# A gated MLP that takes its image by pairs of chunks, in one core of a four-layer network

## The chip, the core and the metric

The kernel runs on one core of one Trainium2 chip. The core has five engines that each take their own list of instructions in the order in which it is written: TensorE (PE; matmuls, with PEld for its weight loads), VectorE (DVE), ScalarE (ACT), GpSimd (POOL), and SyncE (SP), which here only issues DMAs. They wait for each other through semaphores. Data lies in SBUF, 128 partitions wide; matmuls write to PSUM[...].

The metric is the time of one execution on the device in microseconds (us), and its median over runs. All data is float32.

## The reference

Four images of 192 channels and 64 x 64 pixels pass through four layers: L0, an attention over channels with a deformable convolution, and an MLP; L1, an attention over all pixels; L2, an attention in overlapping windows, then a gate and a gated MLP; L3, a convolution with weights made from the image's mean. The change lies in the second half of L2 and touches L3:

```python
out = _hft(_conv1x1(out, proj_w, proj_b), hft_w, hft_b)   # sigmoid(dwconv3(3x - three poolings of x)) * x
x1 = x + out
z = jax.nn.gelu(_conv1x1(_ln_c(x1, n2g, n2b), fc1_w, fc1_b), approximate=False)
z1, z2 = jnp.split(z, 2, axis=1)
z = z1 * _dwconv3(_ln_c(z2, sgn_g, sgn_b), sg_w, sg_b)
return x1 + _conv1x1(z, fc2_w, fc2_b)
```

`_ln_c` is a layer norm over the channels of each pixel, `fc1` goes from 192 to 768 channels, `z1` and `z2` have 384, `_dwconv3` is a 3 x 3 convolution of each channel by itself (nine taps), and `fc2` goes back to 192. L3 then gives each channel four taps of its own image: left, and three of the row above.

## The kernel before, in words

**Order of the whole.** For each image b: `layer1`, with the gathers of image b+1 woven in; `windows` (L2's attention); then `rest(b)`, which runs `project` (the gate `_hft`), `mlp` (the gated MLP) and `layer3`. For images 0 to 2, `rest` also carries `mlp0(b+1)`, L0's MLP of the next image. After `rest`, `keys` and, for some images, `offsets` prepare the next `layer1`.

**How `mlp0` is woven in.** `mlp0` is a generator. It has 33 parts: one to begin, then four for each of 8 chunks. I call them A (`attend` of the next chunk and `widen` of groups 0, 1), B (mean and square of the next chunk's norm, `widen` 2, 3), C (`widen` 4, 5, the norm's variance and reciprocal, `narrow(1)`) and D (the norm's product, `narrow(0)`, the store). `project`, `mlp` and `layer3` yield numbers; each full 1.0 of their sum lets `mlp0` issue its next part there. What is left is issued after `layer3`. Image 3 has nothing beside it (`alone`).

**What sets the order.** Inside `with tc.manual_schedule()`, which encloses the rounds of `mlp`, every engine has the instructions in the order of the program, the parts of `mlp0` that are issued there included. Elsewhere a planner orders them by readiness; it may also put later work, such as `keys`, between the instructions of `mlp`.

**Layout of the image.** `x` holds channels 0 to 127 on the 128 partitions, 4096 pixels long, and channels 128 to 191 on 64 partitions: the upper half of the image (chunks 0 to 3) on partitions 0 to 63, the lower half (4 to 7) on 64 to 127 (`upper_of`). A chunk is 8 rows, 512 pixels, one PSUM bank.

**`project`** works on six units of 1024 elements: units 0 to 3 are channels 0 to 127 of 16 rows each, 4 and 5 the channels above of two halves. `first(u)` projects and pools, `second(u)` does the nine taps, the sigmoid and two products. The halo rows of a unit are copied by POOL, or by two DMAs where they change partitions (`share`).

**`mlp`** goes by chunks, in ten rounds i: chunk i is widened and gated, chunk i+1 is normed, and the taps and the second matmul of chunk i-2 are done. In the order of the code: `taps_of(last, 0)`; `end()` (adds the second matmul of the round before to `x`, with sums for L3); `widen(i, (3, 4, 5))`, which makes `z2` and needs `hns[i]`, the normed chunk; the norm's mean; the gate's mean; the norm's difference and square; the gate's difference and square; `widen(i, (0, 1, 2))` for `z1`; `taps_of(last, 1)`; both variances and reciprocals; `taps_of(last, 2)`; a part of `mlp0`; the norm's product; `gate_scale`, after which ACT writes the gated rows to a strip and POOL copies halo rows (`share`); `narrow(last)`.

`widen` runs, for each of the groups m of 128 output channels, a matmul over 128 rows and one over 64 rows, those of the chunk's half; a matmul of float32 shows in the trace as two records. `narrow` runs three matmuls to 128 and three to 64 output channels. `taps_of` works on 512 columns of DVE: one multiplication and eight multiply-adds, then `z1 = (acc + b) * z1`. In image 3, two of the taps (`GATE_PE`) and five of the gate's in `project` (`HFT_PE`) are matmuls with diagonal matrices.

**PSUM in `rest`.** Tags: `n` (means, broadcasts), 2 banks; `v`, 1; `h` (widening, narrowing, and `mlp0`'s), 5, or in image 3 three, with two for `t` (taps on PE).

Of the kernel before, what the change touches and what calls it, by code (L numbers as in the profile page):

```python
# [79 lines left out]
def conv_seq_kernel(ctx: ExitStack, tc: tile.TileContext, a, out: bass.AP):  # L80
# [1197 lines left out]
    def strips(held):  # L1278


        tiles = {}

        def get(i):
            if i not in tiles:
                t = tiles[i] = held[:, i % held.shape[1]]
                nc.gpsimd.memset(t[:, :, :, 0:1], 0.0)
                nc.gpsimd.memset(t[:, :, :, W + 1 : W + 2], 0.0)
                if i == 0:
                    nc.gpsimd.memset(t[:, :, 0, 1 : W + 1], 0.0)
                if i == NCH - 1:  # L1290
                    nc.gpsimd.memset(t[:, :, 9, 1 : W + 1], 0.0)
            return tiles[i]

        def share(i):

            if i > 0:
                nc.gpsimd.tensor_copy(get(i - 1)[:, :, 9, 1 : W + 1], get(i)[:, :, 1, 1 : W + 1])  # L1297
                nc.gpsimd.tensor_copy(get(i)[:, :, 0, 1 : W + 1], get(i - 1)[:, :, 8, 1 : W + 1])

        return get, share  # L1300

    def depthwise_steps(strip, w, diag, taps, acc, ps, name):


        parts, rows = strip.shape[0], strip.shape[1] - 2
        acc = acc.rearrange("p (r c) -> p r c", c=W)

        def src(tap, r=0, n=rows):
            return strip[:, tap // 3 + r : tap // 3 + r + n, tap % 3 : tap % 3 + W]

        others = [tap for tap in range(9) if tap not in taps]
        first = others.pop(0)
        if taps:
            n = CN // W
            for r in range(0, rows, n):
                p = ps.tile([128, CN], F32, tag="t", name=f"{name}_{r}")[:parts]
                for j, tap in enumerate(taps):
                    nc.tensor.matmul(p, lhsT=diag[:, j, :], rhs=src(tap, r, n), start=j == 0, stop=j == len(taps) - 1)
                to, p = acc[:, r : r + n], p.rearrange("p (r c) -> p r c", c=W)
                nc.vector.scalar_tensor_tensor(to, src(first, r, n), w[:, first : first + 1], p, ALU.mult, ALU.add)  # L1320
        else:
            nc.vector.tensor_scalar_mul(acc, src(first), w[:, first : first + 1])
        for j, tap in enumerate(others):
            nc.vector.scalar_tensor_tensor(acc, src(tap), w[:, tap : tap + 1], acc, ALU.mult, ALU.add)  # L1324
            if j % 3 == 1:
                yield

    def depthwise(*args):
        links(depthwise_steps(*args))


    def upper_of(x, i):

        q, at = i // 4, 4 * UN + CN * (i % 4)
        rows = slice(Q * q, Q * q + Q)
        return x[:, bass.ts(i, CN)], x[rows, at : at + CN], rows

    def chunk_norm_steps(x, i, sb, ps, name):

        lo, hi, rows = upper_of(x, i)  # L1340
        pm = ps.tile([128, CN], F32, tag="n", name=f"pm_{name}")
        nc.tensor.matmul(pm, lhsT=mean_all[:, 0, :], rhs=lo, start=True, stop=False)
        nc.tensor.matmul(pm, lhsT=mean_all[rows, 0, :], rhs=hi, start=False, stop=True)
        yield MEAN
        d = sb.tile([M, 2, CN], F32, tag="ln_d", name=f"d_{name}", bufs=2)
        nc.vector.tensor_tensor(d[:, 0], lo, pm, ALU.subtract)
        nc.vector.tensor_tensor(d[rows, 1], hi, pm[rows], ALU.subtract)
# [405 lines left out]
    class Psums:  # L1753


        def __init__(self, pools):
            self.pools = pools
# [144 lines left out]
```

## Time and profile before

| | us |
|---|---|
| median of 3 runs (lowest, highest) | 7158.63 (7141.57, 7182.09) |
| the profiled execution, its own time | 7071.53 |
| its span, first to last instruction | 7069.4 |
| busy over the span: PE, DVE, ACT, POOL | 6342.5, 4928.1, 3763.7, 2122.6 |
| image 0: `project`, `mlp` | 1858.5 to 2025, 2025 to 2358 |
| image 1: `project`, `mlp`, `layer3` | 3513.7 to 3680, to 4010, to 4041 |
| image 2: `project`, `mlp` | 5170 to 5337, 5337 to 5665 |
| image 3: `project`, `mlp`, `layer3` | 6548 to 6641, to 7035, to 7069.4 |

The stage limits are read from the first and last instructions of the lines that belong to a stage. A stage's row gives, for each engine, its busy time and its number of instructions, then the share of the TensorE clock that was granted (PEclk), the mean share of the DMA engines, and the rate. Matmul records overlap a little, so a busy PE is not a PE at its peak. A row of a group gives line, engine, operation, output and inputs with their shapes, the count; then busy time and mean ns of one; then the idle time just before, and what ended it. A row of the chain gives start, duration, and the work.

### The profile page before, as it was taken

What the parts mean: (1) busy time and instruction counts of PE and PEld (TensorE: products, weight loads), DVE (VectorE), ACT (ScalarE), POOL (GpSimd) and SP (SyncE); (2) the same over time, 40 slices, a digit from 0 to 9 for tenths busy, and PEclk for the clock granted to TensorE, in tenths of its full rate; (3) what the DMA queues carried; (4) which work ended last, traced back from release to release, by engine and by line L of the source; (5) the groups of instructions that cost most, each with busy time, mean ns of one, the idle gap of its engine ahead of it and who ended that gap; (6) DMA issues with size and microseconds to landing.
All of it is one profiled execution on the core that took longest, in us unless ns stands there. A gap on an engine that the chain in (4) does not pass through costs nothing.

```text
span 7069.4 us, 116083 instructions
## 1 busy us (share of the span) xinstructions
PE 6342.5 (90%) x45368; PEld 4236.5 (60%) x45368; DVE 4928.1 (70%) x7476; ACT 3763.7 (53%) x6276; POOL 2122.6 (30%) x2352
## 2 busy tenths in 40 slices
PE   7878999999998799998999699998999889989876
PEld 4545688866553378885654358886654467756332
DVE  3763399955668579984678759994586967746555
ACT  3763388845453268874454258883544345535321
POOL 2761177732100067752200037771200000022100
PEclk8989999989999899998999899998999989989977
DMA  7993367630110377751010167762010010010000
GB/s 239 301 345 102 96 208 228 214 110 12 29 38 3 117 229 218 216 176 36 23 43 7 50 218 227 217 214 60 11 41 25 18 33 12 13 36 7 8 0 19
DMA packets 356994, 742.32 MB, mean 105 GB/s; under 512 B 47463, under 2 KB 241687, under 8 KB 355678
## 3 DMA queue, kind: packets, MB, share of 16 engines
q0 software_dynamic: 95040, 467.22, 20.7%
q1 hardware_dynamic: 261406, 267.69, 12.7%
q8 instruction: 357, 5.85, 0.3%
q14 instruction: 191, 1.56, 0.1%
HBM read 628.06 MB, written 106.21 MB: 104 GB/s over the span
## 4 chain that ended last, share of the span: by engine, by line
PE 45%; DVE 13%; ACT 3%; issue 2%; DMA 1%; POOL 1%; SPq 0%; DVEq 0%; ACTq 0%; POOLq 0%
PE s L910 8%; PE y L976 7%; DVE ga L1324 4%; PE h L590 3%; PE h L1494 3%; PE v L1136 2%; PE qk L1061 2%; PE qk L1062 1%; PE f L1547 1%; PE t L1144 1%; PE po L482 1%; PE zm L1506 1%; PE rb L1210 1%; PE o L818 1%; DVE top L917 1%
## 5 line engine op out<-in xcount | busy, mean ns | idle before, releaser
L572 POOL DMA_INDIRECT ring<-table,idx x1188 | 1696.2, 1428 | 1037.8 <-DMA wkT<-in_wkT_dram 234.6
L910 PE MATMUL s<-ths,ph 96*128 96x256 f32 x4096 | 977.0, 385 | 5.0 <-ACT ths L904 4.0
L910 PEld LDWEIGHTS s<-ths,ph 96*128 96x128 f32 x4096 | 781.8, 192 | 142.4 <-ACT ths L904 16.7
L578 ACT ACTIVATE row<-ring,pos 128x384 f32<-128x384 f32 x1188 | 699.6, 610 | 275.4 <-DVE xo L583 182.7
L579 DVE SCALAR_TENSOR_TENSOR row<-ring,fr,row 128x384 f32<-128x384 f32 x1188 | 700.8, 613 | 126.5 <-ACT row L578 119.8
L976 PE MATMUL y<-sc,gx 128*97 128x256 f32 x3008 | 723.3, 379 | 0.0
L976 PEld LDWEIGHTS y<-sc,gx 128*97 128x97 f32 x3008 | 489.5, 164 | 123.2 <-issue 1.1
L1324 DVE SCALAR_TENSOR_TENSOR ga<-gate,v,ga 128x512 f32<-128x512 f32 x720 | 541.4, 752 | 27.0
L582 ACT ACTIVATE xo<-row,pos 128x192 f32<-128x192 f32 x1188 | 505.3, 448 | 65.4 <-DVE row L579 33.6
L583 DVE SCALAR_TENSOR_TENSOR xo<-row,fr,xo 128x192 f32<-128x192 f32 x1188 | 465.5, 412 | 40.6 <-ACT xo L582 38.1
L590 PE MATMUL h<-ti,xo 128*128 128x192 f32 x2376 | 464.2, 329 | 6.3 <-DVE xo L583 6.3
L912 ACT COPY sc<-s 128x1024 f32<-128x1024 f32 x376 | 377.2, 1003 | 155.7 <-PE s L910 154.6
L973 DVE TENSOR_TENSOR sc<-sc,mbs 128x1024 f32<-128x1024 f32 x376 | 449.1, 1219 | 11.7 <-ACT mbs L936 11.3
L917 DVE TENSOR_TENSOR top<-top,sc 128x1024 f32<-128x1024 f32 x282 | 344.6, 1222 | 127.7 <-ACT sc L912 127.5
L590 PEld LDWEIGHTS h<-ti,xo 128*128 128x128 f32 x2376 | 405.4, 191 | 43.0 <-DVE xo L583 11.2
L974 ACT ACTIVATE sc<-sc 128x1024 f32<-128x1024 f32 x376 | 393.2, 1054 | 29.9 <-DVE sc L973 27.4
L1494 PE MATMUL h<-d_l2n,fc1T 128*128 128x512 f32 (+1 forms) x768 | 375.5, 630 | 34.0 <-DVE x L1555 31.5
L1120 DVE TENSOR_REDUCE es<-ex 128x6 f32<-128x384 f32 x264 | 133.3, 546 | 388.1 <-ACT ex L1116 388.1
L1297 POOL COPY gate<-gate 128x192 f32<-128x192 f32 x28 | 13.9, 497 | 1286.0 <-ACT gate L1528 1286.0
L590 PE MATMUL h<-kept,xo 128*128 128x192 f32 x990 | 253.5, 388 | 80.8 <-DVE xo L583 73.1
L1494 PEld LDWEIGHTS h<-d_l2n,fc1T 128*128 128x128 f32 (+1 forms) x768 | 143.6, 197 | 252.8 <-issue 189.2
L1547 PE MATMUL f<-z,fc2T 128*64 128x512 f32 (+1 forms) x384 | 222.6, 714 | 74.1 <-DVE z L1539 74.1
(376 smaller groups left out, 11409.9 us busy)
## 6 DMA issues: line engine op xcount, KB each, us to landing
ti<-table SPq DMA_DIRECT2D x396, 96.0 KB
table<-tt SPq DMA_DIRECT2D x24, 1056.0 KB
ring<-table,idx POOLq DMA_INDIRECT x1188
xnd<-xn SPq DMA_DIRECT2D x4, 3270.0 KB
table<-kept SPq DMA_DIRECT2D x12, 1056.0 KB
table<-tt SPq DMA_DIRECT2D x44, 288.0 KB
xi<-in_x_dram SPq DMA_DIRECT2D x32, 384.0 KB
xk<-xd SPq DMA_DIRECT2D x32, 384.0 KB
```

Source lines behind the costliest of these rows:

```text
L572: nc.gpsimd.indirect_dma_start(out=gt.rearrange("p r q c -> p (r q c)"), out_offset=None, in_=table[:, :], in_offset=bass.IndirectOffsetOn ...
L578: nc.scalar.activation(row, gt[:, :, 0, :], AF.Copy, scale=pos[:, t, 9 + tap : 10 + tap])
L579: nc.vector.scalar_tensor_tensor(row, gt[:, :, 1, :], fr[:, t, 9 + tap : 10 + tap], row, ALU.mult, ALU.add)
L582: nc.scalar.activation(xo[:, j, :], row[:, 0, :], AF.Copy, scale=pos[:, t, tap : tap + 1])
L583: nc.vector.scalar_tensor_tensor(xo[:, j, :], row[:, 1, :], fr[:, t, tap : tap + 1], xo[:, j, :], ALU.mult, ALU.add)
L590: nc.tensor.matmul(acc[m // 2][:, bass.ts(m % 2, C)], lhsT=xo.rearrange("p j c -> p (j c)")[:, bass.ts(m, 128)], rhs=tt, start=t == 0 and ...
L910: nc.tensor.matmul(p[:, t, :], lhsT=ph[:, bass.ts(G * g + t, 128)], rhs=ths[i], start=True, stop=True)
L917: nc.vector.tensor_tensor(tops[i], tops[i], to, ALU.max)
L973: nc.vector.tensor_tensor(ex, ex, mbs[i].unsqueeze(1).to_broadcast([128, G, QN]), ALU.add)
L976: nc.tensor.matmul(py, lhsT=gx[:, G * g + t, :], rhs=ex[:, t, :], start=g == 0 and t == 0, stop=g == NG - 1 and t == G - 1,)
L1324: nc.vector.scalar_tensor_tensor(acc, src(tap), w[:, tap : tap + 1], acc, ALU.mult, ALU.add)
L1494: nc.tensor.matmul(banks[m], lhsT=fc1b[of, k, bass.ts(m, 128)], rhs=hns[i][of, k, :], start=k == 0, stop=k == 1)
```

## The change

**Pairs.** `of_pair` takes two neighbouring chunks: channels 0 to 127 are 1024 elements of the 128 partitions; channels 128 to 191 of the first chunk lie on partitions 0 to 63 and those of the second on 64 to 127, in the same 512 columns. So `x`, `project`'s units 4 and 5 and the loads of the image are laid out anew. Units 4 and 5 become two blocks of 8 rows each, with halos across the halves of the partitions: 10 DMAs (before: 2 DMAs and two copies by POOL).

**The norm** is done for a pair at once (`pair_norm_steps`): one square, one variance, one root and one reciprocal of twice the size; subtractions and products stay four.

**The taps** run over 16 rows, 1024 columns. `depthwise_steps` is a generator that yields each tap, so that a group's taps are split: `upper_taps` does taps 0 to 5, which don't need the row below, `lower_taps` the last three and the product with `z1`.

**The round.** Five rounds instead of ten; the taps are one pair behind, `narrow` two pairs. The yields are placed anew, in `project` too (three of 0.5 for each `second`, where there were four of 0.83).

**PSUM.** Tag `t` is now `h`: five banks for both, in image 3 too.

```diff
+        yield first
+        for tap in others:
+            for b in range(blocks):
+                nc.vector.scalar_tensor_tensor(acc[:, b], src(tap, b), w[:, tap : tap + 1], acc[:, b], ALU.mult, ALU.add)
+            yield tap
...
+        lo, hi = of_pair(x, j)
+        pms = [ps.tile([128, CN], F32, tag="n", name=f"pm_{name}_{h}") for h in range(2)]
+        for h in range(2):
+            nc.tensor.matmul(pms[h], lhsT=mean_all[:, 0, :], rhs=lo[:, h], start=True, stop=False)
+        for h in range(2):
+            nc.tensor.matmul(pms[h], lhsT=mean_all[half(h), 0, :], rhs=hi[half(h)], start=False, stop=True)
...
+        sq = sb.tile([M, 3, CN], F32, tag="ln_sq", name=f"sq_{name}")
+        nc.scalar.activation(sq, d, AF.Square)
...
+                    moves = [
+                        (lo[:, :, 9, row], hi[:, :, 1, row]), (hi[:, :, 0, row], lo[:, :, 8, row]),
+                        (hi[:, 0, 9, row], lo[:, 1, 1, row]), (lo[:, 1, 0, row], hi[:, 0, 8, row]),
+                    ]
+                    if u == 5:
+                        over = get(4)[half(1), 1]
+                        moves += [(over[:, 9, row], lo[:, 0, 1, row]), (lo[:, 0, 0, row], over[:, 8, row])]
+                    for to, of in moves:
+                        nc.sync.dma_start(out=to, in_=of)
...
                     for _ in second(u):
-                        yield 0.83
+                        yield 0.5
...
+                banks = {(m, h): ps.tile([128, CN], F32, tag="h", name=f"h2_{b}_{j}_{m}_{h}") for m in ms for h in range(2)}
+                for (m, h), p in banks.items():
+                    nc.tensor.matmul(p, lhsT=fc1b[:, 0, bass.ts(m, 128)], rhs=hn[:, h], start=True, stop=False)
+                for (m, h), p in banks.items():
+                    nc.tensor.matmul(p, lhsT=fc1b[half(h), 1, bass.ts(m, 128)], rhs=hn[half(h), 2], start=False, stop=True)
...
+                p = ps.tile([128, CN], F32, tag="h", name=f"f2_{b}_{j}_2")
+                for m in range(3):
+                    for h in range(2):
+                        nc.tensor.matmul(
+                            p[half(h)], lhsT=fc2b[:, m, M:C], rhs=z1[:, m, bass.ts(h, CN)], start=m == 0, stop=m == 2
+                        )
...
+                for j in range(NCH // 2 + 1):
+                    gating, norming, last = j < NCH // 2, j + 1 < NCH // 2, j - 1
+                    lo, hi = 2 * j, 2 * j + 1
+                    if gating:
+                        widen(j, (3, 4))
+                    if last > 0:
+                        narrow(last - 1)
                     if last >= 0:
+                        upper_taps(last, 0)
                     end()
+                    if last >= 0:
+                        yield 1.0
+                    if not gating:
+                        lower_taps(last, 0)
+                        yield 1.0
+                    if gating:
+                        widen(j, (5, 0))
+                    if last >= 0:
+                        upper_taps(last, 1)
+                    if not gating:
+                        lower_taps(last, 1)
+                        yield 1.0
+                    yield 1.0
+                    if gating:
+                        gate_mean(lo)
+                        gate_mean(hi)
+                        gate_difference(lo)
+                        gate_square(lo)
+                        gate_difference(hi)
+                        widen(j, (1, 2))
+                        gate_variance(lo)
+                        gate_square(hi)
+                    if last >= 0:
+                        upper_taps(last, 2)
                     if not gating:
                         yield 1.0
+                        lower_taps(last, 2)
+                        yield 2.0
                     if gating:
+                        nc.vector.reciprocal(r[lo], r[lo])
+                        if last >= 0:
+                            yield 1.0
+                        gate_variance(hi)
+                        gate_scale(lo)
+                        nc.vector.reciprocal(r[hi], r[hi])
+                    if gating:
+                        if last >= 0:
+                            lower_taps(last, 0)
+                        gate_scale(hi)
                     if norming:
+                        norm = pair_norm_steps(x, j + 1, sb, ps, f"l2n2_{b}_{j + 1}")
+                        links(norm, SQUARE)
                     if gating:
+                        if last >= 0:
+                            lower_taps(last, 1)
                         yield 1.0
                     if norming:
+                        links(norm, INVERSE)
                     if gating:
+                        if last >= 0:
+                            lower_taps(last, 2)
                     if norming:
+                        hns[j + 1] = links(norm)
+                    hns.pop(j, None)
+                narrow(NCH // 2 - 1)
                 end()
...
-            wide = s.enter_context(pool_of(name="restps2", bufs=3 if alone else 5, space=PSUM))
-            psums = Psums({"n": ps, "v": ps, "t": ps, "h": wide})
+            wide = s.enter_context(pool_of(name="restps2", bufs=5, space=PSUM))
+            psums = Psums({"n": ps, "v": ps, "h": wide}, {"t": "h"})
```

In the round, the removed lines (the ten rounds told above) are left out. `layer3` follows the new layout: for units 4 and 5 a tap is three DVE instructions (7 rows of each block, and the two first rows together), where it was one, or two for unit 4.

## The prediction

> **What bounds the kernel now.** The chain that ended last (part 4 of the page) is 45% TensorE (PE) and 13% VectorE (DVE) over the whole program. The change touches only the end of each image, so the next view is the busy time by stage: `project` and `mlp` of image 1, two rounds of that `mlp`, then `project` and `mlp` of image 3, beside which no `mlp0` runs.
>
> ```profile
> core 0: us, PE busy (x) PEld busy (x) DVE busy (x) ACT busy (x) POOL busy (x), PEclk, DMA share, GB/s
> 3513.70:3680.00 166.30, 156.06 (x763) 87.74 (x762) 135.97 (x206) 83.82 (x123) 5.35 (x16) 0.98 0.17 48
> 3680.00:4010.00 330.00, 292.64 (x1264) 141.21 (x1263) 258.36 (x366) 124.40 (x178) 12.46 (x43) 0.95 0.07 19
> 3815.85:3887.20 71.35, 63.74 (x282) 29.39 (x281) 64.63 (x91) 29.07 (x39) 2.98 (x8) 0.95 0.02 6
> 6548.00:6641.00 93.00, 82.39 (x212) 34.25 (x212) 65.11 (x114) 25.53 (x29) 18.10 (x37) 0.92 0.03 7
> 6641.00:7035.00 394.00, 299.52 (x884) 120.54 (x884) 219.89 (x293) 97.85 (x127) 6.60 (x29) 0.80 0.01 2
> ```
>
> `project` is PE-bound through the work beside it: by tiles, `mlp0` is 125 of its 156 us of PE and 33 of its 136 us of DVE. In `mlp` of images 0 to 2 PE (89%) and DVE (78%) share the bound; 61 us of that PE and 14 of that DVE are `mlp0`, 25 of PE the next image's `keys`. A middle pair takes 71.4 us with DVE busy for 64.6: there DVE sets the pace. In image 3 neither engine is full and PE's clock is 0.80: waits bind it.
>
> The groups by shape, the chain, and the waits of image 3's `mlp` give the sizes:
>
> ```profile
> L1324 DVE SCALAR_TENSOR_TENSOR ga<-gate,v,ga 128x512 f32<-128x512 f32 x192 | 144.3, 752 | 7.2
> L1324 DVE SCALAR_TENSOR_TENSOR ha<-hft,wide,ha 128x1024 f32<-128x1024 f32 x32 | 40.8, 1275 | 0.5
> ```
> ```profile
> 3600.43 1.73 PE h L796 x8
> 3602.15 1.11 PE h L803 x8
> 3617.28 2.74 PE o L821 x24
> 3815.85 5.54 PE h L1494 x12
> 3887.21 5.54 PE h L1494 x12
> 6788.84 9.20 PE h L1494 x10
> 6806.06 5.34 PE h L1494 x12
> ```
> ```profile
> PE h L1494 <- DVE x L1555: 31.5, 5, 6.3
> ```
>
> From start to start in the chain a tap takes 0.785 us at 512 columns and 1.31 at 1024. In image 3 a round takes 44 to 53 us (292 for six); after a wait of 6.3 us, ten records of L1494 take 9.2 us, twice their 0.45 each.
>
> [...] eight 64-row records that alternate halves (L803) take 1.11 us against 1.73 for full ones, and 24 that alternate column halves (L821) 0.114 each against 0.216. The old gated MLP's 64-row matmuls stay on one half and cost a full 0.43 each. [...] 0.785 and 1.31 leave 0.26 fixed. [...]
>
> **The change part by part.**
>
> *Work, per image.* PE: `widen` has 24 64-row records a pair, x 0.43 x 0.36 saved (1 - 1.11/1.73) = 3.7 us; `narrow` 12 x 0.43 x 0.47 (1 - 0.114/0.216) = 2.4; the norm's mean 0.6: four pairs, -27. DVE: a channel group of a pair took 2 x (0.46 + 9 x 0.785) = 15.1, now 0.75 + 9 x 1.31 = 12.5; 12 groups, -30. Three sums for four in `end`: -3. `project`'s units 4 and 5 now go in two blocks of 8 rows, 2 x (0.46 + 8 x 0.785) against 0.75 + 8 x 1.31: +2.2 each. Net -28. (Image 3, two taps on PE: -22 in `mlp`.) ACT: one square and one root of the norm for two, off the path. SP: ten halo DMAs for two; only `second(4)` and `second(5)` wait for them, about 2 us each, as before; mlp0's loads queue behind them on SP but are issued a chunk ahead. Uncovered they would cost 2 us an image. Layer 3: a tap of units 4 and 5 goes from 1.27 us to 0.69 + 0.69 + 0.35 (448 and 128 columns, by the 0.26 fixed), six of them, where DVE is the path: +2.
>
> *Where `mlp0` goes.* Yields come to 11 in `project` (22 before) and 21 in `mlp` (16). `project` then holds a third of the 33 parts: DVE 136 - 33 + 16 + 4 = 123 us, PE 31 + 62 = 93. DVE is its bound; it was busy 97 to 100% of the old `project` from 3600 to 3660, so 128 us: **-38**. A middle round of `mlp` gets four parts (23 us PE, 6 DVE), a pair before had two; two parts are left for layer 3.
>
> *The new round, images 0 to 2.* Each engine takes its instructions in the written order. I walk through it with the trace's durations; t = 0 is the first product of `hn`. PE is busy from 0 to 41 us; the times are ends:
>
> ```
> PE   widen(3,4) 5.3 | narrow 13.2 | D 19.4 | widen(5,0) 24.7 | A 30.2 | means 35.4 | widen(1,2) 40.7
> DVE  products 2 | upper 0 9.4 | end 14.2 | D 20.3 | upper 1 27.6 | A 28.7 | differences 37.2 | upper 2 44.5
>      reciprocal 45.5 | B 47 | scale lo 49.6 | reciprocal 52.5 | lower 0 59.8 | scale hi 61.5
>      norm's differences 66.3 | lower 1 71.5 | C, reciprocals 77 | lower 2 82 | product 83
> ```
>
> DVE waits 4 us for D's `narrow(0)`, 4 for the first mean, 2 for the second root (on ACT behind B's gelus and their table load), 2 for `lower_taps(0)`'s halo row (three ACT rows of 0.8 after the scale, then POOL's copy), 2 for the norm's second mean (it needs the `n` bank that scale hi frees), 2 for C (its gelus stand behind the norm's square), and the rest at banks and hand-overs: 63 us of work in 83. Behind `lower_taps(0)` stand scale hi and the norm, on which PE waits, so PE idles from 56 on. The same walk through an old round gives 34.2 where 35.7 was measured; 86 then.
>
> Without taps, round 0 is 55 us by the same walk. The last round, with seven parts between its taps, then `narrow` (7.9) and three sums (2.6) that nothing covers, is 72. `mlp`: 55 + 3 x 86 + 72 = 385 against 330, **+55**. The saved 27 us of PE and 28 of DVE lie within it; the two more parts a pair take back 11 us of PE each.
>
> *Behind it.* `mlp0` ended before the last rounds and `keys` (30 us PE) ran under their taps. Now two parts (11 us) and `keys` come under layer 3, where PE idles 30 us, and after it: **+8** (bounds 0, if all is hidden, and +25). With layer 3's **+2**, images 0 to 2 take -38 + 55 + 2 + 8 = +27 each, +81.
>
> *Image 3.* Five shared banks for three end the 6.3 us wait of L1494, but `widen(5,0)` needs four while `narrow` holds three until `end`, and the taps of group 0 wait for PE until 15 us (23 at half clock). The walk gives 88 a pair, half clock in its first 15 us as measured, against 97: -28. Round 0: -7. The tail: +14, since `narrow`, taps and sums of a whole pair stand open there. **-21**. All: 81 - 21 = **+60**.
>
> On the profiled execution's own 7071.5 that is 7132; the median of runs lies 87 above it, so the same step gives 7158.6 + 60 = **7219**.
>
> **Rivals.** *Faster: DVE has no gaps.* Place: rounds 1 to 3. If the queues run further ahead than I walked, work decides: 63 us of DVE and 60 of PE make a round of 72; that is 3 x 3 x 14 = 126 less, and 8 less in each last round: 60 - 150 = -90, **7070**. It decides under 75 us a round. For: the old pair has DVE at 90%. Against: old image 3, where each step of the chain lies open. *No difference:* rounds of 79, 60 - 63, **7155**. *Slower still:* PE idles 9 us near t = 60; if half clock then lasts 15 us as in image 3, each round is 6 longer, 60 + 54: **7273**. *The packing does not pack* (accumulating pairs run one by one): PE +7 a pair, 16 pairs, half of it under DVE, + 54: **7273**.
>
> **How the numbers follow.** Forecast 0.36, packing failure 0.06, slower still 0.12, no difference 0.19, faster 0.27. Below 0.5% (36 us) a change can't be told from none: the runs of before spread over 41. Slower is 0.54, the first three. The likeliest case alone: 7195 to 7260. Eight in ten needs both signs: 7085, with 0.12 below, to 7285, with 0.07 above.
>
> **What would show it.** Right: `project` near 128 us with DVE over 90%; `mlp` of images 0 to 2 near 385 with both engines under 77%, and DVE waiting for the mean, for part D and for POOL before `lower_taps(0)`; taps of 1.28 us; 64-row records at about 0.26; `keys` after layer 3 begins; `mlp` of image 3 near 375. Wrong: rounds near 72, or PE over 90% in `mlp`: then parts did not stand in the way as walked.

## The result, and the profile after

The changed kernel takes 7163.44 us (median of 20 runs, 7134.05 to 7186.77), the kernel before, on the same chips, 7143.85 (20 runs). The ratio is 1.0021, with a 95% interval from 1.0004 to 1.0038: about 20 us more. The interval only just leaves out no change at all, and the executions of one kernel spread over more than that: 53 us here, 65 before. The prediction was +60 us.

The profiled execution took 7177.11 us with a span of 7175.2. It can't be set against the 7069.4 of before as a whole. The stages that the change does not touch, up to the end of image 0's windows, already differ by 91 us (1858.5 and 1949.5); 71 of them lie in the first gathers, ahead of the first `mlp0` (600.4 and 671.3). So all comparisons here go by stage. Each image is cut at four places: the end of its windows, the first record of `widen`, the last sum of `end`, and the first attention matmul (L910) of the next `layer1`, or the end of the program.

| us, before / after | `project` | `mlp` | from there to the next `layer1` | all |
|---|---|---|---|---|
| image 0 | 167.3 / 125.3 | 331.5 / 370.0 | 145.0 / 149.2 | 643.9 / 644.5 |
| image 1 | 166.7 / 125.5 | 329.4 / 370.6 | 142.5 / 155.6 | 638.7 / 651.7 |
| image 2 | 167.2 / 125.1 | 327.3 / 370.6 | 38.3 / 84.7 | 532.8 / 580.4 |
| image 3 | 92.5 / 94.8 | 393.2 / 347.8 | 34.8 / 36.0 | 520.5 / 478.6 |

The last column's differences add up to +19.3 us, close to what the medians differ by (19.6); each column is from one profile. So a small difference hides large ones of both signs: +61 in images 0 to 2, -42 in image 3.

The busy time by stage of the changed kernel, in the order of the rows of before: `project` and `mlp` of image 1, a middle round, `project` and `mlp` of image 3.

```profile
core 0: us, PE busy (x) PEld busy (x) DVE busy (x) ACT busy (x) POOL busy (x), PEclk, DMA share, GB/s
3610.90:3736.50 125.60, 102.32 (x422) 55.09 (x421) 116.90 (x197) 54.73 (x73) 4.40 (x12) 0.87 0.16 45
3736.50:4107.10 370.60, 304.06 (x1323) 155.32 (x1322) 247.15 (x257) 132.19 (x196) 3.96 (x21) 0.88 0.05 14
3877.60:3962.50 84.90, 71.05 (x307) 35.41 (x307) 60.25 (x63) 30.66 (x44) 0.65 (x2) 0.88 0.05 15
6696.60:6791.30 94.70, 83.95 (x216) 35.22 (x216) 69.89 (x127) 25.76 (x28) 15.89 (x31) 0.93 0.05 14
6791.30:7139.10 347.80, 237.65 (x785) 101.89 (x784) 195.06 (x192) 78.72 (x104) 3.39 (x9) 0.78 0.00 1
```

In `project` VectorE is now the busiest engine (117 of 126 us). A middle round, with four parts of `mlp0` in it, takes 84.9 us with VectorE at 71% and TensorE at 84% of it, where the old pair took 71.4 with VectorE at 91%. PE's clock in `mlp` fell from 0.95 to 0.88.

Of VectorE's waits in that middle round, these are four that the prediction had named (us in total, times, the longest):

```profile
DVE z L1516 <- PE zm L1512: 6.0, 2, 5.2
DVE d_l2n L1326 <- PE pm_l2n L1322: 4.2, 1, 4.2
DVE xa L825 <- PE o L818: 3.7, 1, 3.7
DVE ga L1304 <- POOL gate L1542: 1.6, 1, 1.6
```

In this order it waits for the gate's mean, for the norm's mean, for part D's second matmul, and for the halo row ahead of `lower_taps(0)`. Its other waits there, for `narrow`'s matmuls above all, are 8 us together. The groups by shape in `mlp` of image 1 show the long taps and the 64-row matmuls:

```profile
L1304 DVE SCALAR_TENSOR_TENSOR ga<-gate,v,ga 128x1024 f32<-128x1024 f32 x64 | 82.3, 1287 | 6.9 <-POOL gate L1542 4.8
L1503 PE MATMUL h<-d_l2n,fc1T 64*128 64x512 f32 x96 | 23.8, 615 | 0.0
```

96 records of 64 rows occupy 23.8 us, 0.25 each, and their starts lie in pairs, 0.01 us apart (3882.77 and 3882.78, 3883.30 and 3883.31 in the middle round): here they run two at a time.

What stands between the end of image 2's `mlp` and `layer1(3)` is read from the chain. Before, where `keys` (L858, L863) begins among the last `narrow`s (L1547):

```profile
5630.26 5.51 PE f L1547 x8
5635.77 1.03 PE tp L858 x2
5636.80 1.76 PE g L863 x16
...
5702.78 17.07 PE s L910 x64
```

After, where it begins behind `mlp0`'s last sum, two stores of `layer3` (L1757) and its own first load:

```profile
5801.25 0.66 DVE xa L825
...
5802.70 0.61 SPq L1757
...
5803.36 0.60 SPq L1757
...
5804.06 5.38 DMA xk<-xd
5809.49 3.73 PE tp L858 x4
5813.22 3.36 PE g L863 x16
...
5857.43 12.79 PE s L910 x58
```

All of `keys` stands bare there: 48 us from its first record (L858) to L910. Most of it runs at half clock: 16 records of L863 take 3.36 us for 1.76. The trace's own record of the clock, which in these traces knows only full and half, has it at half from 5795.7 to 5846.9 us. TensorE had been idle for 18.7 us ahead of `keys`, from 5790.8 us on, and the fall lies 4.9 us into that; but then it is busy without a break for 37 us, and the clock stays at half through all of them:

```profile
5809.50:5857.40 47.90, 47.32 (x164) 31.23 (x164) 4.46 (x8) 5.93 (x9) 0.00 (x0) 0.61 0.19 56
```

Why it came back so late is open. In the kernel before, `keys` began at half clock too, behind 4.9 us of idleness, but had full clock 5.6 us later.

### The profile page after: what moved, and what is told of

The parts are those of the page before. It is cut to its first block, busy times and chain, and to the rows that moved or that the text cites. A ratio compares the mean times of both kernels' runs of the same rounds, so it can differ in the third digit from the quotient of the medians.

```text
span 7175.2 us, 114768 instructions
## 1 busy us (share of the span) xinstructions
PE 6303.2 (88%) x44984; PEld 4274.4 (60%) x44984; DVE 4833.2 (67%) x7096; ACT 3700.7 (52%) x6194; POOL 2080.4 (29%) x2256
## 4 chain that ended last, share of the span: by engine, by line
PE 64%; DVE 16%; ACT 7%; issue 4%; DMA 4%; SPq 1%; POOL 1%; another core or an unknown queue 1%; ACTq 0%; DVEq 0%; POOLq 0%
PE s L910 11%; PE y L976 11%; PE h L590 6%; PE h L1501 2%; PE v L1136 2%; PE qk L1061 2%; DVE ha L1304 2%; PE qk L1062 2%; PE o L818 1%; PE t L1144 1%; DVE ga L1304 1%; DMA ring<-table,idx 1%; PE zm L1512 1%; PE rb L1210 1%; PE tp L858 1%
## 5 line engine op out<-in xcount | busy, mean ns | idle before, releaser
L910 PE MATMUL s<-ths,ph 96*128 96x256 f32 x4096 | 979.3, 385 | 12.0 <-ACT ths L904 4.4
L910 PEld LDWEIGHTS s<-ths,ph 96*128 96x128 f32 x4096 | 783.1, 193 | 150.1 <-ACT ths L904 13.1
L1120 DVE TENSOR_REDUCE es<-ex 128x6 f32<-128x384 f32 x264 | 133.3, 546 | 370.3 <-ACT ex L1116 370.3
L1304 DVE SCALAR_TENSOR_TENSOR ga<-gate,v,ga 128x1024 f32<-128x1024 f32 x240 | 308.8, 1287 | 27.7 <-POOL gate L1542 19.9
L590 PEld LDWEIGHTS h<-kept,xo 128*128 128x128 f32 x990 | 192.4, 227 | 207.7 <-DVE xo L583 111.6
L976 PE MATMUL y<-se,gx 128*97 128x256 f32 x1088 | 259.2, 379 | 0.5 <-ACT yn L982 0.5
L1184 POOL TENSOR_TENSOR ot<-ot,ot 102x128 f32<-102x128 f32 x80 | 55.9, 711 | 622.2 <-ACT ot L1178 621.9
```

The costliest lines, as they stand in the source:

```text
L590: nc.tensor.matmul(acc[m // 2][:, bass.ts(m % 2, C)], lhsT=xo.rearrange("p j c -> p (j c)")[:, bass.ts(m, 128)], rhs=tt, start=t == 0 and ...
L910: nc.tensor.matmul(p[:, t, :], lhsT=ph[:, bass.ts(G * g + t, 128)], rhs=ths[i], start=True, stop=True)
L976: nc.tensor.matmul(py, lhsT=gx[:, G * g + t, :], rhs=ex[:, t, :], start=g == 0 and t == 0, stop=g == NG - 1 and t == G - 1,)
L1304: nc.vector.scalar_tensor_tensor(acc[:, b], src(tap, b), w[:, tap : tap + 1], acc[:, b], ALU.mult, ALU.add)
```

## The experiments

Three questions came out of the table. Where do the gains of image 3 and of `project` come from? What did late parts of `mlp0` cost? And why does a round take 85 us, when both engines have less work to do?

**Parts of `mlp0` early again, in the new kernel.**

```diff
                     for _ in second(u):
-                        yield 0.5
+                        yield 0.83
```

> The changed kernel with project's yields at 0.83 for 0.5: 17 parts of mlp0 in project for 11, so the 33rd part comes after the second of the last round's seven places. Theory: the new kernel loses its gain behind mlp, where keys wait for the last parts of mlp0. Then in images 0 to 2 project is some 9 us longer (six parts at 1.5 us of VectorE), the last round of mlp some 10 shorter, keys of image 2 run under the last round and layer 3, and the stretch from the end of mlp to layer1(3) falls from 85 us to about 40. In all -50 to -80, near 7090. Rival: project, where VectorE is the bound already, takes back what the end gives, and keys stay behind layer 3: within 15 us of the changed kernel.

Measured: ratio to the kernel before 0.9963 (0.9948 to 0.9978), median 7128.91. From end of `mlp` to `layer1(3)`: 48.1 us for 84.7; `project` +20 to +22, `mlp` of images 0 to 2 -21 to -25. Image 2 falls from 580.4 to 539.0, images 0 and 1 by 4 and 11. The theory holds in place and sign. But six more parts cost `project` 3.5 us each, not 1.5 (VectorE is busy for 131 us there for 117), and the gain is 41 us by the ratios (0.9963 against 1.0021), less than the 50 to 80 expected.

**The same in image 2 alone**, `yield 0.5 if b < 2 else 0.83`:

> The changed kernel with project's yields at 0.83 in image 2 alone. Theory: the 47 us that image 2 lost behind its windows are keys that stand bare before layer1(3): image 2 gets back 35 to 45 us, the others nothing: -40 against the changed kernel. Rival: they come from the gated MLP itself: within 10.

Measured: 0.9959 (0.9936 to 0.9981), median 7126.11; image 2 takes 540.7 us for 580.4, images 0 and 1 stay at 645.1 and 644.4. The chain now shows `keys` around the last `narrow` (L1571), its first records at half clock and the later ones of these lines at full:

```profile
5746.60 3.73 PE tp L858 x4
5750.33 3.36 PE g L863 x16
5753.69 4.86 PE f L1571 x8
5758.55 2.73 PE f L1576 x12
5761.27 1.89 PE tp L858 x4
```

So image 2 gets back 40 of the 47 us that it lost, 37 of them behind `mlp`, where `keys` had stood bare (48.1 us for 84.7).

**Parts of `mlp0` late, in the kernel before.**

```diff
                     for _ in second(u):
-                        yield 0.83
+                        yield 0.5
```

> The kernel before with project's yields at 0.5 for 0.83: 14 parts of mlp0 in project for 22, sixteen in mlp, three left for layer 3. Theory: late parts cost the old kernel what they cost the new one: project 166 to about 140 us, mlp 330 to about 355, and the stretch from mlp's end to layer1(3) in image 2 from 38 to about 80; in all +40. Rival: the place of the parts does not matter, only the rounds do: within 15 us of the kernel before.

Measured: 0.9986 (0.9974 to 0.9999), median 7148.59. `project` fell to 141.4 us, as expected, but the old `mlp` took up what was moved to it almost free. Image 1:

```profile
core 0: us, PE busy (x) PEld busy (x) DVE busy (x) ACT busy (x) POOL busy (x), PEclk, DMA share, GB/s
3590.00:3731.30 141.30, 111.36 (x515) 61.34 (x514) 124.04 (x186) 60.75 (x86) 5.02 (x16) 0.91 0.12 37
3731.30:4063.80 332.50, 299.41 (x1292) 143.77 (x1292) 263.77 (x375) 129.06 (x189) 11.71 (x40) 0.95 0.05 14
```

332.5 us for 329.4. So images 0 and 1 gain 24 and 19 us (643.9 to 619.7, 638.7 to 620.0), and image 2 loses 35 (532.8 to 567.6) by `keys`: 92.8 us behind `mlp` for 38.3. The theory of the bare `keys` holds, its sum does not: by the stages the yields alone are worth -8. And 25 of the 41 us that the change gained in `project` do not need pairs; the yields of `project` come to 14 parts here and to 11 in the changed kernel, and the rest was not tested by itself.

**Five shared banks in image 3, in the kernel before.**

```diff
-                p = ps.tile([128, CN], F32, tag="t", name=f"{name}_{r}")[:parts]
+                p = ps.tile([128, CN], F32, tag="h", name=f"{name}_{r}")[:parts]
...
-            wide = s.enter_context(pool_of(name="restps2", bufs=3 if alone else 5, space=PSUM))
-            psums = Psums({"n": ps, "v": ps, "t": ps, "h": wide})
+            wide = s.enter_context(pool_of(name="restps2", bufs=5, space=PSUM))
+            psums = Psums({"n": ps, "v": ps, "h": wide})
```

> The kernel before, where in image 3 the taps on TensorE and the widening share five PSUM banks (three and two before). Theory: image 3 gained 41 us mostly by its banks, which end the wait of 6.3 us a round: -25 to -40 in image 3, nothing elsewhere. Rival: image 3 gained by less work and fewer hand-overs (half as many rounds, packed matmuls, long taps): -10 to 0.

Measured: 0.9915 (0.9899 to 0.9931), median 7090.86, which is 64 us below that of the kernel before. Image 3 takes 453.0 us for 520.5. Its `mlp`, and two rounds of it:

```profile
core 0: us, PE busy (x) PEld busy (x) DVE busy (x) ACT busy (x) POOL busy (x), PEclk, DMA share, GB/s
6725.30:7048.40 323.10, 258.04 (x884) 107.75 (x884) 218.56 (x288) 97.72 (x127) 6.42 (x29) 0.91 0.01 3
6808.40:6883.10 74.70, 64.10 (x230) 27.66 (x229) 53.88 (x72) 24.48 (x32) 1.49 (x8) 0.95 0.00 0
```

The five waits of L1494 for a bank, 31.5 us in the prediction's row, are gone, and the same 884 matmul records take 258 us for 299.5, at a clock of 0.91 for 0.80. Both together, 73 us, are about the 70 that `mlp` lost: each of these waits cost its length, 6.3 us, and some 8 more, a fifth of the 41.5 us that the matmul records took longer. In the kernel before, half clock begins inside each of the five waits and lasts 7 to 21 us; with shared banks these stretches are gone, and of `mlp` 58 us are at half clock for 157. A pair of chunks takes 74.7 us, against 97 before and 87.6 in the changed kernel's full round. The gain is larger than the theory's, and image 3 with pairs and banks (478.6) is 26 us slower than with the banks alone.

**Both, put where they gain:** the kernel before with the shared banks, and `yield 0.5 if b < 2 else 0.83` in `project`.

> The kernel before with five shared banks in image 3, and project's yields at 0.5 in images 0 and 1 and 0.83 in image 2. Theory: the parts of the sum are independent: -61 from the banks, -24 and -19 from images 0 and 1 as the stages of the two runs with one edit each show, nothing in image 2: -100 against the kernel before, near 7050. Rival: the 61 us were partly another length of the gathers (the stages of image 3 show 67 of it, so this is not likely), or parts left behind layer 3 delay the offsets of images 2 and 3: -60.

Measured: 0.985 (0.9822 to 0.9879), median 7039.67. Images 0 to 3 take 620.5, 622.6, 532.3 and 459.3 us, 101 less in all: the parts add up as the theory says, but for 6 us in image 3, where the clock was 0.87 in `mlp` and 0.91 with the banks alone. This kernel is faster than both, and it has neither pairs nor long taps.

**What packing is worth.** First only the order of neighbours: in `widen` the two 64-row matmuls of chunk lo, then the two of hi; in `narrow` the three of lo, then the three of hi.

> The changed kernel with the same matmuls in another order: in widen the 64-row matmuls of one half of the rows after those of the other, in narrow those of one half of the columns after the other, so that neighbours lie on the same half. Theory: 24 records in widen and 12 in narrow go from 0.25 and 0.23 us to 0.43, +6.7 us of TensorE for each of 16 pairs; in a round TensorE works without a break for its first half while VectorE waits for it, so most of it is on the path: +70 to +107. Rival: TensorE idles 14 us of a round of 85 and takes it up there: 0 to +30.

Measured: 1.0057 (1.0038 to 1.0077), median 7200.28: 0.4% above the changed kernel; `mlp` +5.4, +4.9, +4.7 and +2.3 us. But the trace shows that the edit undid little. In `widen`, eight records (four matmuls) still take 1.99 us, and their starts lie in pairs, 0.01 us apart, though two matmuls of lo stand ahead of two of hi. In `narrow`, where six records stand in a row, twelve take 3.71 us for 2.80. So this run says nothing of packing's worth. The next one keeps the halves apart:

```diff
-                for (m, h), p in banks.items():
-                    nc.tensor.matmul(p, lhsT=fc1b[:, 0, bass.ts(m, 128)], rhs=hn[:, h], start=True, stop=False)
-                for (m, h), p in banks.items():
-                    nc.tensor.matmul(p, lhsT=fc1b[half(h), 1, bass.ts(m, 128)], rhs=hn[half(h), 2], start=False, stop=True)
+                for h in range(2):
+                    for m in ms:
+                        nc.tensor.matmul(banks[m, h], lhsT=fc1b[:, 0, bass.ts(m, 128)], rhs=hn[:, h], start=True, stop=False)
+                    for m in ms:
+                        nc.tensor.matmul(banks[m, h], lhsT=fc1b[half(h), 1, bass.ts(m, 128)], rhs=hn[half(h), 2], start=False, stop=True)
...
-                p = ps.tile([128, CN], F32, tag="h", name=f"f2_{b}_{j}_2")
-                for m in range(3):
-                    for h in range(2):
+                    if h == 0:
+                        ps2.append(ps.tile([128, CN], F32, tag="h", name=f"f2_{b}_{j}_2"))
+                    p = ps2[0]
+                    for m in range(3):
                         nc.tensor.matmul(
                             p[half(h)], lhsT=fc2b[:, m, M:C], rhs=z1[:, m, bass.ts(h, CN)], start=m == 0, stop=m == 2
                         )
```

> The changed kernel with the 64-row matmuls of the two halves apart: in widen and in narrow, full matmuls stand between those of one half and those of the other. Theory: nothing packs then: 24 records in widen and 12 in narrow take 0.43 us for 0.25 and 0.23, +6.7 us of TensorE for each of 16 pairs, 107 in all; most of it lies in the first half of a round, where TensorE sets the pace: +60 to +107 against the changed kernel. Rival: the hand-overs cover it: 0 to +30.

Measured: 1.0176 (1.0148 to 1.0204), median 7288.52. The 64-row groups in `mlp` of image 1:

```profile
L1504 PE MATMUL h<-d_l2n,fc1T 64*128 64x512 f32 x96 | 50.1, 643 | 0.0
L1579 PE MATMUL f<-z,fc2T 128*64 128x512 f32 x48 | 23.9, 636 | 0.0
```

50.1 for 23.8, 23.9 for 11.2: 39 us more of TensorE an image, and 0.52 and 0.50 us a record for 0.25 and 0.23. `mlp` grows by 37.7, 32.6, 32.2 and 25.2 us, and the whole by 111 us by the ratios, a little above the range. The theory holds: in images 0 to 2 nearly all of it is on the path, in image 3 most.

**What long taps are worth.** Here each tap goes over twice 512 columns instead of once 1024, the halves in turn.

```diff
-                nc.vector.scalar_tensor_tensor(acc[:, b], src(tap, b), w[:, tap : tap + 1], acc[:, b], ALU.mult, ALU.add)
+                n = 8 if name[:2] == "gt" else rows
+                for r in range(0, rows, n):
+                    to = acc[:, b, r : r + n]
+                    nc.vector.scalar_tensor_tensor(to, src(tap, b, r, n), w[:, tap : tap + 1], to, ALU.mult, ALU.add)
```

> The changed kernel with each multiply-add of the gated MLP's taps in two of 512 columns instead of one of 1024. It adds 12 groups x 8 taps x 0.26 us = 25 us of VectorE to each of images 0 to 2 and 19 to image 3, 94 in all. Theory: the first six taps of a group lie where VectorE waits for TensorE anyway, the last three on the path: some 9 us an image, +30 to +45 against the changed kernel. Rival: all taps are on the path: +80 to +95. Second rival: the round is bound by TensorE and hand-overs alone: 0 to +15.

Measured: 1.0032 (1.0019 to 1.0044), median 7159.77; `mlp` 367.9, 366.4, 366.9 and 347.8 us, the same as with long taps or less. But VectorE did not get the 94 us: from start to start a half takes 0.6625 us, two of them 1.325 where a long one takes 1.320. In the old kernel a tap of 512 took 0.787. Two things had changed at once: here an instruction does not read what the one before it wrote. So the next run does all taps of one half, then all of the other. The first line is of this run, the second of that one:

```profile
L1307 DVE SCALAR_TENSOR_TENSOR ga<-gate,v,ga 128x512 f32<-128x512 f32 x480 | 323.6, 743 | 14.2 <-POOL gate L1545 13.1
L1307 DVE SCALAR_TENSOR_TENSOR ga<-gate,v,ga 128x512 f32<-128x512 f32 x480 | 355.2, 750 | 16.5 <-POOL gate L1550 2.9
```

> The changed kernel with each group's taps in two runs of 512 columns, all taps of one half before those of the other (an earlier run alternated the halves tap by tap, and a tap took 2 x 0.6625 us from start to start, as much as one of 1024 columns). Theory: what a short tap lost in the old kernel was not its number of instructions but that it adds to what the instruction before it wrote: now 0.785 again for 512 columns, 1.57 a tap for 1.32, 24 us of VectorE in each of images 0 to 2 and 18 in image 3. On the time: three of eight taps lie in the half of a round where VectorE sets the pace: +30 to +45; if all are on the path +85. Rival: 0.6625 again, since the old 0.785 came from something else (the strips' layout): nothing.

Measured: 1.0044 (1.0027 to 1.006), median 7185.28. From start to start it is 0.78 to 0.79 us again in 493 of the 629 cases where two of these taps stand next to each other; most of the others lie where one half gives way to the other. `mlp` is 370.3, 372.3, 372.9 and 354.0 us: at most 2.3 more in images 0 to 2, 6.2 in image 3. The same middle round as above now has 64.7 us of VectorE in it for 60.3:

```profile
3879.50:3964.50 85.00, 70.90 (x309) 35.69 (x307) 64.73 (x86) 30.78 (x44) 1.19 (x2) 0.90 0.05 14
```

It lasts 85.0 us, as long as before. VectorE's wait for POOL falls from 1.6 to 0.2 us, since half by half the upper half's last taps need no halo row, and its wait for the gate's mean from 6.0 to 4.8; over all its waits 5 us go, and these make up for the added work. So the VectorE time that long taps save was worth little in images 0 to 2: 0.3 to 2.3 us an image. Against the changed kernel the run is 16 us slower by the ratios (1.0044 less 1.0021, times 7144); 10 of them are in `mlp` by the stages, 6 of these in image 3. The expected +30 to +45 did not come.

**What makes a round long.** The next pair's norm, up to its square, is issued ahead of the gate's reciprocals instead of behind `gate_scale(hi)`:

```diff
                     if last >= 0:
                         upper_taps(last, 2)
+                    if norming:
+                        norm = pair_norm_steps(x, j + 1, sb, ps, f"l2n2_{b}_{j + 1}")
+                        links(norm, SQUARE)
...
                         gate_scale(hi)
-                    if norming:
-                        norm = pair_norm_steps(x, j + 1, sb, ps, f"l2n2_{b}_{j + 1}")
-                        links(norm, SQUARE)
```

> The changed kernel with the next pair's norm (mean, differences, square) issued right after upper_taps of group 2 instead of after gate_scale of the second chunk. Theory: a round is long because its chain stands open at the end: scale, bank, mean of the next pair, differences, square, with TensorE idle for 5 us and VectorE for 4 while it waits for that mean. Then each of rounds 0 to 2 loses 5 to 7 us in all four images: -50 to -80 against the changed kernel. Rival: the wait only moves (to the product of the scale, or to ACT's queue, where the square now stands ahead of the gate's root): -10 to +15.

Measured: 1.0003 (0.9985 to 1.0022), median 7135.2. `mlp` of image 3 falls from 347.8 to 333.8 us, that of images 0 to 2 by 2.3, 3.2 and 1.1. The theory holds in sign where `mlp0` is not beside it; elsewhere the rival does. By the ratios the whole gains 13 us. Then the rest of the norm is moved up too, right behind `gate_scale(hi)`:

> As the run before it, and the norm's variance, root, reciprocal and product come right after gate_scale of the second chunk, ahead of lower_taps of groups 1 and 2 and of the last part of mlp0. Theory: then TensorE starts the next round's widening while VectorE still does the last six long taps: 8 us more covered in each of rounds 0 to 2: -90 to -150 against the changed kernel. Rival: VectorE now stands at the head of its queue waiting for the norm's root with the taps behind it, so the wait comes back as VectorE's: within 20 us of the run before it.

Measured: 0.9964 (0.9949 to 0.9979), median 7111.07: `mlp` 362.9, 363.8, 363.4 and 334.0. 7 us an image there, and 41 in all by the ratios, for 90 and more expected. Last, on top of it, two of a middle round's four parts of `mlp0` go from its first half to its second:

```diff
                     end()
-                    if last >= 0:
+                    if last >= 0 and not gating:
                         yield 1.0
...
-                    yield 1.0
+                    if last < 0 or not gating:
+                        yield 1.0
...
                         if last >= 0:
+                            yield 1.0
                             lower_taps(last, 0)
...
                         if last >= 0:
+                            yield 1.0
                             lower_taps(last, 1)
```

> As the kernel with all of the next norm issued early, and two of the four parts of mlp0 in a middle round move from its first half (behind end and behind upper_taps of group 1) to its second half (ahead of lower_taps of groups 0 and 1). Theory: a round has a first half bound by TensorE (some 41 us of its work beside 24 of VectorE) and a second bound by VectorE (44 us beside 30 of TensorE); two parts are 10 us of TensorE in the first half: the middle rounds of images 0 to 2 go from 83 us to 73 to 77, in all -40 to -80 against the kernel with the norm early; image 3 stays. Rival: the parts' own waits on VectorE and ACT in the second half cost as much as they free, or the halves are not the bound: -10 to +20.

Measured: 0.9926 (0.9897 to 0.9955), median 7102.68; `mlp` 353.5, 352.6 and 350.3 us, image 3 unchanged at 334.0. From one first gate mean to the next it is 80.0 and 79.0 us in image 1 where `narrow` lies between (82.7 and 82.2 in the run before it, 85.0 and 85.1 in the changed kernel), and 54.5 where it does not, from round 0 to round 1 (66.2 and 67.5). These 12 us are no gain of their own: the stretch has lost two parts to a later one, while each of the two full stretches still holds four. There, 10 us of TensorE's work moved out of the first half took some 3 us off the round. By this run that half, in which TensorE works through `narrow`, D, `widen`, A and the means, sets a round only in small part. By the ratios the run gains 27 us on the one before it, for the 40 to 80 expected: PE now waits 11.9 us for the norm's reciprocal, which stands on VectorE behind a moved part (9.0 in the run before). What a round's remaining 80 us are bound by was not settled.

**The sum of it.** Take from each image what the old kernel gains or loses by the yields alone and by the banks alone; what is left is the pairs, with their packing, long taps and new round:

| us | image 0 | image 1 | image 2 | image 3 | sum |
|---|---|---|---|---|---|
| parts late (kernel before, yields 0.5) | -24.2 | -18.7 | +34.8 | 0 | -8.1 |
| shared banks (kernel before) | 0 | 0 | 0 | -67.5 | -67.5 |
| the rest: pairs | +24.8 | +31.7 | +12.8 | +25.6 | +94.9 |
| the change | +0.6 | +13.0 | +47.6 | -41.9 | +19.3 |

Each figure is from one profile, and image 3 of the kernel with late parts, whose code is that of before, took 511.0 us for 520.5: figures of image 3 are good to some 10 us. The third row is the remainder, not a run: it takes the edits as independent, and it also holds the three parts of `mlp0` by which the yields of `project` differ (14 and 11). It holds packing, which alone is worth 25 to 38 us an image in `mlp`, 128 in all; without it, by these sums, the pairs would be some 220 us behind. The order of the round costs two thirds of what is left: with the norm early and the parts moved, the images take 628.2, 627.5, 569.6 and 464.9 us, against 619.7, 620.0, 567.6 and 453.0 of the old rounds with late parts and shared banks: 30 us in all for 95.

## Why the prediction was wrong

The sum was made step by step, so each can be set against the stages. Two steps failed above all. A full round's time was multiplied by three, in all four images, though only one round is full: some 20 us too much an image. And `keys` was taken to be covered by `layer3`: 34 us too little, nearly all of it in image 2.

**`project`, -38:** right in place and nearly in size: -42.0, -41.2 and -42.1, with VectorE busy for 93% of it. The prediction also saw that this work is moved, not gone.

**`mlp` of images 0 to 2, +55:** +38.5, +41.2 and +43.3. The walk came out close: a middle round with everything in it takes 84.9 us for the 86 forecast, and VectorE waits where it was to wait: 5.2 us for the gate's mean, 3.7 for part D, 4.2 for the norm's mean, 1.6 for POOL. In part this is luck: the walk took full clock where 0.88 was granted, and a round of 80 us in a reordered kernel could not be accounted for. The last round was 68.5 for 72. What failed is the factor in "3 rounds x 86". Only one round has both a `narrow` and a norm: the one after the first has no `narrow`, the one before the last no norm. They took 75.9 and 76.1, together 20 us less than two full ones; that the missing pieces make this difference is read from the code, not from a run that adds them. Round 0 was 65.2 for 55; the granted clock was 0.84 there, and the walk had taken it at full speed, but how much of the 10 us that makes was not tried. With the last round that is -20 + 10 - 4 - 1 = -15, from 385 to 370.6. That both engines would be under 77% was wrong for PE (82%, at a clock of 0.88).

**Layer 3 and what lies behind, +2 and +8 (bounds 0 to +25):** +4.2, +13.1 and +46.4. This step was most wrong in image 2. The prediction saw that `keys` would come late, and let its 30 us run under `layer3`, where PE idles. But the loads of `keys` stand in SyncE's list behind the last store of `mlp0`. That store was issued at 5801.9 us, once the part's sum was done, and the sum stands in VectorE's list among the taps of `layer3`. Behind it come two stores of `layer3`, and only then the first load, which takes 5.4 us. It starts 2.1 us after that store was issued, as soon as SyncE comes to it, and fetches chunk 0, which an earlier part had stored: it was held by its place in SyncE's list. So none of `keys` ran under `layer3`, and most of it ran at half clock: 48 us. In images 0 and 1 `offsets` stands at the same place anyway, `keys` overlaps it (in image 1 from 4143 to 4199, `offsets` from 4148 to 4258), and little is lost. The upper bound of 25 was too low: it had `keys` at 30 us, where they took 48.

**Image 3, -21:** -41.9, and -45.4 in `mlp` itself. The full round took 87.6 us, as walked (88), but again the two beside it are short (73.0 and 79.4), together 24 us less than two of 88: as much as `mlp` was off. And the reasoning gave the rounds' gain to pairs and banks together. The run with banks alone shows -67.5 without pairs: what the pairs do in image 3 is, as the difference of the two, a loss of 26.

**Work saved.** PE: sizes right (64-row records at 0.25, forecast 0.26), and worth more than I said. The packing's failure was priced at half its PE time, +54; it would have been some 110 (1.0176 against 1.0021). DVE: long taps take 1.287 us as forecast, but the 0.26 us "fixed" cost, an estimate from 0.785 and 1.31, is in two halves in these runs: 512 columns take 0.6625, and 0.125 more (0.787) where an instruction reads what the one before it wrote. So the two blocks of `project`'s units 4 and 5, whose taps alternate and start every 0.6625 us, cost some 0.3 us a unit more by an estimate from these starts, where +2.2 was forecast. That VectorE's saving would lie under its own waits was right.

**The rivals.** "No difference" is where the time fell, but not by its mechanism (rounds of 79): the full rounds did not get shorter than walked. "DVE has no gaps" is excluded by the waits and by a round that stays at 85.0 us with 4.5 more of VectorE in it. "Slower still" is there in part: the granted clock of a middle round is 0.88, and the first eight records of L1501 take 5.3 us in it where eight later ones take 3.6; but the round did not grow past 86 by it. So the walk, which knew no half clock in images 0 to 2, came out right in its sum and must be too long in some of its parts.

**Together.** The +60 was wrong by terms of both signs, which in part cancel by luck: in `mlp` of images 0 to 2 -42 (123 for 165), in `project` -11 (-125 for -114), behind `mlp` +34 (64 for 30), in image 3 -21. Their sum is -40, which takes +60 to about +20.

## What to carry to other kernels

When a change bundles an edit of buffers, one of placement and one of the work itself, make each small one alone first: here the two small ones, put where they gain, bring the time to 0.985 of that before, and the large one costs what they bring. Count how many rounds of a loop really have every piece in them, before a round's time is multiplied. And where work is moved later, follow what stands behind its last piece, through each engine's list and SyncE's too, and if PE idles ahead of it, price it at half clock as well: here that held for 37 us of steady work behind 18.7 us of idleness, and for 5.6 us behind 4.9.

## What the runs showed of the hardware that was not expected

- A chain of multiply-adds on VectorE that each read what the one before wrote takes 0.787 us at 512 columns and 1.320 at 1024, from start to start. Where two such chains alternate it is 0.6625 (the halves in turn) and 1.195 (in the old `project`, where the taps of two units alternate, as in the three lines below). So, by these differences, 0.125 us of each is the dependence, and 0.13 the instruction. In the trace of before, each chained tap of L1324 at 512 columns also waits for a semaphore that VectorE's own instructions update, and 0.035 us lie between the end of one tap and the start of the next (0.787 less its own 0.752). What of the 0.125 us is that wait was not parted. In these runs what looked like one cost of 0.26 us has two parts, and alternating two chains took away the one for the dependence.

```profile
3601.04 1.28 DVE L1324 SCALAR_TENSOR_TENSOR ha<-hft,wide,ha 128x1024 f32<-128x1024 f32 x1
3602.23 1.28 DVE L1324 SCALAR_TENSOR_TENSOR ha<-x,wide,ha 128x1024 f32<-128x1024 f32 x1
3603.43 1.28 DVE L1324 SCALAR_TENSOR_TENSOR ha<-hft,wide,ha 128x1024 f32<-128x1024 f32 x1
```

- 64-row matmuls on the two halves of the rows took no longer when two of the one half stood ahead of two of the other in the program: eight records take 1.99 us in either order, and 4.18 with full matmuls between the halves (50.1 us for 96). With three matmuls in a row on each column half twelve records take 3.71 us for 2.80, and 5.98 with full ones between (23.9 us for 48). The trace doesn't name the halves; that it is records of the two halves that overlap is inferred from these times.
- Five waits of 6.3 us for a bank cost image 3 of the kernel before 70 us in `mlp`, 14 each: more than half of it, 41.5 us, is that the same matmul records took longer (157 us of that stage at half clock, 58 without the waits).
- Half clock outlasted the idleness by far in two runs. In the changed kernel `keys` of image 2 ran at half clock for its first 37 us, with PE busy in every one of them, behind 18.7 us of idleness. In the kernel before with late parts it ran so for all of its 57 us (PE busy for 56.1), behind 12.6. What brings the clock back was not found.
